# Two layers of graph attention on one core: loading and turning h earlier in the order of issue

## The chip, the cores and the metric

The kernel runs on one core of one Trainium2 chip. The metric is the device time of a launch in microseconds (us). Before the change it was 4149.87 us, the median of three runs from 4149.01 to 4151.54.

A core has engines that each work through a queue of their own in order: TensorE (PE) for matmuls, VectorE (DVE), ScalarE (ACT), GpSimd (POOL), and SyncE (SP), which issues most DMAs here. They wait for one another by semaphores. The kernel fixes the order in each queue itself: an operation's place in the program is its place in its engine's queue.

## The reference, cut to what matters

There are 32 batches of 512 rows by 512 features. Layer 0 adds a graph sum to x and normalises; layer 1 adds masked attention with eight heads and normalises again.

```python
def _L0(x, adj, W, b):
    Wi, Wj = W[:, :512], W[:, 512:]
    mi = einsum('bkd,od->bko', x, Wi); mj = einsum('bkd,od->bko', x, Wj)
    a = adj.astype(x.dtype); deg = a.sum(axis=1)
    return deg[None, :, None] * (mi + b) + einsum('ij,bjo->bio', a, mj)

def _L1(h, adj, ...):                        # 8 heads of 64
    q, k, v = [split_heads(h @ Wx.T + bx) for x in "qkv"]
    scores = einsum('bhqd,bhkd->bhqk', q, k) / 8
    scores = where(adj == 0, -inf, scores)
    out = einsum('bhqk,bhkd->bhqd', softmax(scores), v)
    return merge_heads(out) @ Wo.T + bo

x = layernorm(x + _L0(x, adj, ...))          # this is h
x = layernorm(x + _L1(x, adj, ...))
```

## The kernel before

Each large product is done in 2 by 2 blocks with seven products instead of eight. Such a product is a **piece**; its number i (1 to 7) says which of the seven it is. Pieces 1, 2 and 3 take quarters of the activations as they are; pieces 5, 6, 7 and 4 take differences of quarters (t1 to t4), which GpSimd makes. The kinds of piece are `l0` (layer 0's two products), `v`, `q`, `k`, and `pj` (the output projection). The weights' blocks come from DRAM through a ring of eight tiles: after each piece, `prefetch` issues the load of the tiles that the ring has room for, and that load waits until the piece has read its own.

```python
def piece(kind, b, i, bank):
    ...
        a = {1: (0, 0), 2: (1, 0), 3: (1, 1)}.get(i)
        terms.append((take((name, i)), quarters(*a) if a else T[:, {5: 0, 6: 1, 7: 2, 4: 3}[i]]))
    ...                                       # matmuls into PSUM (L413)
    prefetch()                                # ring loads, issued by SyncE
    ...                                       # the result's way out of PSUM, ACT or DVE
```

In the loop over n, the periods, three batches are under way at once: batch n has layer 0's product and normalisation and then v, q, k; batch n - 1 has its attention; batch m = n - 2 has its projection and second normalisation. Layer 0's result h must be had transposed for v, q and k. From n = 2 on this goes through DRAM: `h_store` writes h (issued by ScalarE), `h_load` reads it back in blocks of 32 columns (four DMAs, issued by SyncE), and `h_turn` transposes inside blocks of 32 by 32 on VectorE. All three work by halves; a half is two of the four groups of 128 rows.

```python
def stats(b, half):                           # DVE: bn_stats, bn_aggr; POOL: three small operations
    for ic in range(2 * half, 2 * half + 2):
        MV[b, ic] = work([P, 5], "mv", 12)
        ln_stats(MV[b, ic], XT[b][:, ic, :])
# apply(b, half): ScalarE scales and shifts the same rows

def h_store(b, half):
    if half == 0:
        HR[b] = dram.tile([N, D], FT, name="hd", bufs=2)
    nc.scalar.dma_start(rows(HR[b])[:, 2 * half:2 * half + 2, :], XT[b][:, 2 * half:2 * half + 2, :])

def h_load(b, half):
    if half == 0:
        HA[b] = work([P, DC, N], "xa", 1).rearrange(...)
    src = HR[b].rearrange("(t p) (c q f) -> q p c t f", p=32, q=4, f=32)
    for q in range(4):
        nc.sync.dma_start(HA[b][32 * q:32 * q + 32, half].rearrange("p c (t f) -> p c t f", f=32),
                          src[q][:, :, 8 * half:8 * half + 8, :])

def h_turn(b, half):
    if half == 0:
        HT[b] = big()
    nc.vector.transpose(HT[b][:, :, Q * half:Q * half + Q], HA[b][:, half])
```

The quarters with second index 0 lie in h's first half. So v 1, v 2, q 1, q 2, k 1 and k 2 need the first turn alone, and the differences `combos(TH, ...)`, hence q 5 and v 5, need both.

A period is cut into eight steps of about equal TensorE time (`by_steps`). Each step begins with the attention of batch n - 1, for half a head pair: scores, exponentials on ScalarE, masks on VectorE, then the values of the step before. After that come the step's pieces, with what is left of the attention dealt out between them: `presum` (sums of exponentials, the first on GpSimd, the next two on VectorE), `invert` (reciprocals on VectorE), `scale`, and `tell` (one row of a check of ranges, called told below).

```python
def scores(b, hp, kc):
    ...                                       # matmuls of k and q (L467)
    nc.scalar.activation(ps, ps, AF.Exp, scale=QSCALE)
    nc.vector.tensor_tensor(e, ps, edge[...], op=OP.mult)     # the mask, L472

def presum(hp, half):
    if half == 0:
        ES[hp] = work([P, 2, N], "es", 1)
        nc.gpsimd.tensor_add(ES[hp], E[0], E[1])              # L478
    else:
        nc.vector.tensor_add(ES[hp], ES[hp], E[half])         # L480
```

With n = 10 the old order gives these steps (worked out from the lists; `combTH` are the differences of h):

```
2  apply(10,0) h_store(10,0) l0.5 add_bo(9,1) pj.4 h_load(10,0) l0.3 stats(10,1) stats(8,0) pj.5
3  h_turn(10,0) apply(10,1) h_store(10,1) v.1 pj.3 stats(8,1) v.2 q.1 h_load(10,1) k.1 apply(8,0) apply(8,1) q.2
4  store(8) k.2 h_turn(10,1) combTH combTH q.5 v.5 q.3 v.3
```

## Time and profile before

| | |
|---|---|
| device time | 4149.87 us, median of 3 |
| span of the profiled execution | 4152.1 us |
| mean granted TensorE clock | 0.953 of full |
| one batch in the middle of the run | about 128 us |
| DMA | 127 GB/s over the span |

The page is read like this. Times are in us. PE is TensorE's matmuls, PEld its weight loads, DVE VectorE, ACT ScalarE, POOL GpSimd, SPq and ACTq the DMA issues of SyncE and ScalarE. In a line of a timeline, an idle time in brackets stands ahead of the operation, and "<-" names what ended it; "issue" means that the profile shows no releaser. A tile named `big` holds turned activations or differences, `ring` a weight block, `mma` and `mmb` are two PSUM banks, `oT` is the attention's output, `xa` h as loaded and not yet turned, `hd` its copy in DRAM.

The costliest groups of instructions by engine:

```profile
L413 PE MATMUL mma<-ring,big 128*128 128x256 f32 x3112 | 770.4, 399 | 74.7 <-issue 70.8
L472 DVE TENSOR_TENSOR e<-sc,edge 128x1024 f32<-128x1024 f32 x512 | 602.5, 1218 | 360.2 <-ACT sc L471 360.2
L382 POOL TENSOR_TENSOR big<-big 128x512 f32<-128x512 f32 x376 | 507.4, 1377 | 28.6 <-ACT big L340 12.0
L413 PE MATMUL mmb<-big,ring 128*128 128x256 f32 x1776 | 451.0, 399 | 44.1 <-POOL big L382 44.1
```

The first number after the bar is the group's busy time in us, the second the mean of one in ns; then the idle time just before the group's members and what ended most of it.

### The profile page before, as it was taken

What the parts mean: (1) busy time and instruction counts of PE and PEld (TensorE: products, weight loads), DVE (VectorE), ACT (ScalarE), POOL (GpSimd) and SP (SyncE); (2) the same over time, 40 slices, a digit from 0 to 9 for tenths busy, and PEclk for the clock granted to TensorE, in tenths of its full rate; (3) what the DMA queues carried; (4) which work ended last, traced back from release to release, by engine and by line L of the source; (5) the groups of instructions that cost most, each with busy time, mean ns of one, the idle gap of its engine ahead of it and who ended that gap; (6) DMA issues with size and microseconds to landing.
All of it is one profiled execution on the core that took longest, in us unless ns stands there. A gap on an engine that the chain in (4) does not pass through costs nothing.

```text
span 4152.1 us, 46000 instructions
## 1 busy us (share of the span) xinstructions
PE 3881.7 (93%) x16426; PEld 2653.3 (64%) x16426; DVE 2695.3 (65%) x3580; ACT 989.1 (24%) x1356; POOL 2027.5 (49%) x1985
## 2 busy tenths in 40 slices
PE   9999999999999999999999999999999999999987
PEld 6666666666666666666666666666666666666653
DVE  4666666667666676666666666666667666666665
ACT  2222222222222222222222222222222222222222
POOL 3545553455544555445554455553455544555432
PEclk9999999999999999999999999999999999999998
DMA  7444445544445344454444444444534445444441
GB/s 236 124 125 119 129 126 132 140 122 124 120 135 140 115 124 125 131 140 125 118 126 131 132 135 122 124 120 135 144 112 125 126 128 142 117 122 128 130 114 39
DMA packets 803720, 529.25 MB, mean 127 GB/s; under 512 B 529568, under 2 KB 626336, under 8 KB 803488
## 3 DMA queue, kind: packets, MB, share of 16 engines
q1 hardware_dynamic: 786912, 494.26, 43.6%
q10 hardware_dynamic: 16320, 31.46, 2.0%
q8 instruction: 135, 2.21, 0.2%
q14 instruction: 97, 0.79, 0.1%
q0 software_dynamic: 256, 0.53, 0.0%
HBM read 453.25 MB, written 72.88 MB: 127 GB/s over the span
## 4 chain that ended last, share of the span: by engine, by line
PE 85%; issue 4%; DVE 4%; ACT 4%; POOL 3%; DMA 0%; SPq 0%; ACTq 0%; POOLq 0%; DVEq 0%
PE mma L413 28%; PE mmb L413 28%; PE sc L467 10%; PE ov L488 10%; PE mmb L311 3%; PE mma L311 3%; ACT xh L282 2%; PE ov L495 2%; DVE e L472 2%; POOL es L478 2%; POOL big L382 1%; ACT sc L471 1%; ACT q L456 1%; DVE rl L510 0%; PE ov L505 0%
## 5 line engine op out<-in xcount | busy, mean ns | idle before, releaser
L471 ACT ACTIVATE sc<-sc 128x1024 f32<-128x1024 f32 x512 | 492.8, 1006 | 1761.0 <-PE sc L467 1757.1
L413 PE MATMUL mma<-ring,big 128*128 128x256 f32 x3112 | 770.4, 399 | 74.7 <-issue 70.8
L472 DVE TENSOR_TENSOR e<-sc,edge 128x1024 f32<-128x1024 f32 x512 | 602.5, 1218 | 360.2 <-ACT sc L471 360.2
L413 PE MATMUL mmb<-ring,big 128*128 128x256 f32 x3144 | 759.4, 392 | 74.7 <-issue 72.2
L413 PEld LDWEIGHTS mma<-ring,big 128*128 128x128 f32 x3112 | 617.4, 200 | 219.3 <-issue 98.2
L413 PEld LDWEIGHTS mmb<-ring,big 128*128 128x128 f32 x3144 | 610.6, 196 | 211.6 <-issue 99.9
L194 POOL TENSOR_TENSOR xlo<-xh,xhi 128x512 fp32r<-128x512 f32 x128 | 215.3, 1692 | 736.6 <-ACT xhi L193 736.6
L382 POOL TENSOR_TENSOR big<-big 128x512 f32<-128x512 f32 x376 | 507.4, 1377 | 28.6 <-ACT big L340 12.0
L467 PE MATMUL sc<-q,k 64*128 64x512 f32 x2048 | 510.0, 616 | 0.0
L488 PE MATMUL ov<-e,v 128*64 128x512 f32 x2048 | 496.9, 606 | 4.2 <-DVE oT L520 4.2
L413 PE MATMUL mma<-big,ring 128*128 128x256 f32 x1808 | 455.0, 397 | 45.4 <-POOL big L382 44.7
L413 PE MATMUL mmb<-big,ring 128*128 128x256 f32 x1776 | 451.0, 399 | 44.1 <-POOL big L382 44.1
L510 DVE RECIPROCAL rl<-ov 128x128 f32<-128x128 f32 x512 | 466.1, 933 | 11.4 <-PE ov L505 5.7
L478 POOL TENSOR_TENSOR es<-e 128x1024 f32<-128x1024 f32 x128 | 301.9, 2359 | 339.9 <-DVE e L472 219.5
L413 PEld LDWEIGHTS mma<-big,ring 128*128 128x128 f32 x1808 | 354.3, 198 | 128.5 <-POOL big L382 51.2
L413 PEld LDWEIGHTS mmb<-big,ring 128*128 128x128 f32 x1776 | 349.2, 199 | 126.5 <-POOL big L382 50.1
L277 POOL TENSOR_SCALAR mv<-mv 128x1 f32<-128x1 f32 x256 | 49.5, 193 | 774.9 <-DVE mv L276 762.3
L480 DVE TENSOR_TENSOR es<-es,e 128x1024 f32<-128x1024 f32 x248 | 357.8, 1443 | 0.0
L488 PEld LDWEIGHTS ov<-e,v 128*64 128x64 f32 x2048 | 124.6, 136 | 344.4 <-issue 271.8
L467 PEld LDWEIGHTS sc<-q,k 64*128 64x128 f32 x2048 | 176.7, 186 | 208.1 <-issue 208.1
L431 DVE TENSOR_TENSOR xh<-xh,mma 128x512 f32<-128x512 f32 x186 | 126.0, 677 | 277.4 <-PE mma L413 276.8
L431 DVE TENSOR_TENSOR xh<-xh,mmb 128x512 f32<-128x512 f32 x186 | 126.0, 677 | 254.9 <-PE mmb L413 254.8
(144 smaller groups left out, 3774.4 us busy)
## 6 DMA issues: line engine op xcount, KB each, us to landing
ring<-wq SPq DMA_DIRECT2D x160, 256.0 KB, 2.7
ring<-wv SPq DMA_DIRECT2D x160, 256.0 KB, 2.6
ring<-wk SPq DMA_DIRECT2D x160, 256.0 KB, 2.8
ring<-wi SPq DMA_DIRECT2D x155, 256.0 KB, 2.8
ring<-wj SPq DMA_DIRECT2D x155, 256.0 KB, 2.7
ring<-wo SPq DMA_DIRECT2D x155, 256.0 KB, 2.7
xh<-in_x_dram SPq DMA_DIRECT2D x32, 1024.0 KB, 5.5
xa<-in_x_dram SPq DMA_DIRECT2D x124, 256.0 KB, 4.0
```

The costliest lines, as they stand in the source:

```text
L194: nc.gpsimd.tensor_sub(lo, xs, hi.bitcast(FT))
L311: nc.tensor.matmul(pm, parts[w][:, jc, :], adjR[:, jc, :], start=(w == 0 and jc == 0), stop=(w == 1 and jc == NC - 1))
L382: nc.gpsimd.tensor_tensor(dst, p, q, op=OP.subtract)
L413: nc.tensor.matmul(pm[:, c * Q:(c + 1) * Q], lhs, rhs, start=first, stop=(kc == 1 and n == len(terms) - 1), skip_group_check=True)
L431: nc.vector.tensor_tensor(d, d, pm, op=OP.add)
L467: nc.tensor.matmul(ps[:, s, :], KT[b, hp // 2][r, hp % 2, kc * P:(kc + 1) * P], QT[b, hp // 2][r, hp % 2, :], start=True, stop=True)
L471: nc.scalar.activation(ps, ps, AF.Exp, scale=QSCALE)
L472: nc.vector.tensor_tensor(e, ps, edge[:, kc:kc + 1, :].to_broadcast([P, 2, N]), op=OP.mult)
L478: nc.gpsimd.tensor_add(ES[hp], E[0], E[1])
L480: nc.vector.tensor_add(ES[hp], ES[hp], E[half])
L488: nc.tensor.matmul(PV[hp][s * HD:(s + 1) * HD, :], V[b][:, kc, c0:c0 + HD], E[kc][:, s, :], start=(kc == 0), stop=(kc == NC - 1))
L510: nc.vector.reciprocal(rl[:, c], pl[:, c])
```

## The change

Only the order of issue changes, for the batches n = 2 to 31. The first load of h stands directly after piece l0 5, so that SyncE reaches it ahead of the ring tiles that piece pj 4 sets free; the second stands after pj 3 instead of after q 1. The first turn stands ahead of piece pj 5 and thus of the next step's masks; the second, and the differences made from it, stand ahead of k 2, and thus of a reciprocal and of GpSimd's sum. The statistics of batch m move behind pj 3. The purpose is to have h turned sooner for v, q and k.

```diff
-                *project(m, 7), z(apply, n, 0), z(h_store, n, 0), l0[5], z(add_bo, n - 1, 1), *project(m, 4), z(h_load, n, 0),
-                l0[3], z(stats, n, 1), z(stats, m, 0), *project(m, 5)]
+                *project(m, 7), z(apply, n, 0), z(h_store, n, 0), l0[5], z(h_load, n, 0), z(add_bo, n - 1, 1), *project(m, 4),
+                l0[3], z(stats, n, 1), z(h_turn, n, 0), *project(m, 5)]
 ...
-            res = [z(h_turn, n, 0), z(apply, n, 1), z(h_store, n, 1), v[1], *project(m, 3), z(stats, m, 1), v[2], q[1],
-                   z(h_load, n, 1), k[1], z(apply, m, 0), z(apply, m, 1), q[2], z(store, m), k[2], z(h_turn, n, 1),
-                   z(combos, TH, n, h, (1, 2)), z(combos, TH, n, h, (3, 4))]
+            res = [z(apply, n, 1), z(h_store, n, 1), v[1], *project(m, 3), z(h_load, n, 1), z(stats, m, 0), v[2], z(stats, m, 1),
+                   q[1], k[1], z(apply, m, 0), q[2], z(apply, m, 1), z(store, m), z(h_turn, n, 1),
+                   z(combos, TH, n, h, (1, 2)), z(combos, TH, n, h, (3, 4)), k[2]]
```

## The prediction

> **What bounds the kernel now.** I began with the page's busy line and then the chain of waits, by engine:

> ```profile
> PE 3881.7 (93%) x16426; PEld 2653.3 (64%) x16426; DVE 2695.3 (65%) x3580; ACT 989.1 (24%) x1356; POOL 2027.5 (49%) x1985
> ...
> PE 85%; issue 4%; DVE 4%; ACT 4%; POOL 3%; DMA 0%; SPq 0%; ACTq 0%; POOLq 0%; DVEq 0%
> ```

> TensorE is the bound, and the other 15% of the chain is waiting that TensorE does. To find where, I read TensorE's timeline for one batch in the middle of the run (columns: start, duration, engine, line, output and inputs, count, and in brackets the idle time before and its releaser):

> ```profile
> 2054.80 1.99 PE L467 MATMUL sc<-q,k 64*128 64x512 f32 x8
> 2056.72 1.94 PE L488 MATMUL ov<-e,v 128*64 128x512 f32 x8
> 2063.37 3.75 PE L413 MATMUL mma<-ring,big 128*128 128x256 f32 x8 [4.71 <-issue]
> 2066.92 2.34 PE L413 MATMUL mmb<-ring,oT 128*128 128x256 f32 x8
> 2069.09 1.89 PE L413 MATMUL mma<-ring,big 128*128 128x256 f32 x8
> ...
> 2076.09 1.99 PE L467 MATMUL sc<-q,k 64*128 64x512 f32 x8
> ...
> 2080.74 1.99 PE L413 MATMUL mma<-big,ring 128*128 128x256 f32 x8
> 2085.67 3.78 PE L413 MATMUL mmb<-big,ring 128*128 128x256 f32 x8 [2.94 <-POOL big L382]
> 2089.25 3.11 PE L413 MATMUL mma<-ring,big 128*128 128x256 f32 x8
> ...
> 2095.74 1.99 PE L467 MATMUL sc<-q,k 64*128 64x512 f32 x8
> ```

> Two holes, 4.71 and 2.94 us. The windows of 130 us around them have TensorE busy 122.35 us, so 7.65 us idle: these two are all the idle time of a batch. The same two stand in every batch from n = 2 on whose timeline I looked at, with the same lengths. The first eight-matmul piece after each takes 3.75 us instead of 1.89. The views by window give the reason (the two columns to read are TensorE's busy time, the first, and PEclk, the granted clock, third from the end of the line):

> ```profile
> 2059.00:2060.00 1.00, 0.00 (x0) 0.00 (x0) 1.00 (x4) 0.68 (x1) 0.81 (x3) 1.00 0.00 0
> 2060.00:2061.00 1.00, 0.00 (x0) 0.00 (x0) 1.00 (x2) 0.00 (x0) 0.84 (x3) 1.00 0.39 150
> 2061.00:2062.00 1.00, 0.00 (x0) 0.00 (x0) 1.00 (x1) 0.00 (x0) 0.27 (x2) 0.50 0.98 373
> ...
> 2066.00:2067.00 1.00, 1.00 (x4) 0.75 (x3) 0.00 (x0) 0.00 (x0) 0.00 (x0) 0.50 0.00 0
> ```

> TensorE stops at 2058.66 (2056.72 + 1.94). At about 2061.0, after 2.3 us of idling, its clock falls to half and stays there until about 2067.8. A hole costs its length and then half of the slow time after it. VectorE is 1.00 busy throughout.

> Next I asked what ends each hole: VectorE's and GpSimd's timelines, and SyncE's queue of DMA issues.

> ```profile
> 2059.76 2.35 DVE L472 TENSOR_TENSOR e<-sc,edge 128x1024 f32<-128x1024 f32 x2
> 2062.03 1.24 DVE L359 STREAM_TRANSPOSE big<-xa 128x1024 f32<-128x1024 f32 x1
> ...
> 2082.68 1.19 DVE L359 STREAM_TRANSPOSE big<-xa 128x1024 f32<-128x1024 f32 x1
> ```
> ```profile
> 2082.05 2.35 POOL L478 TENSOR_TENSOR es<-e 128x1024 f32<-128x1024 f32 x1 [7.57 <-DVE e L472]
> 2084.36 5.04 POOL L382 TENSOR_TENSOR big<-big 128x512 f32<-128x512 f32 x4
> ```
> ```profile
> 2050.20 3.24 SPq L353 DMA_DIRECT2D xa<-hd  x4
> ```

> Hole 1: the turn of h's first half ends at 2063.27 and v's first piece starts at 2063.37; the releaser named "issue" is really this turn. Its data were not late: the four loads issue from 2050.20, and the last (at about 2052.5, 3.9 us to landing) is there at 2056.4. The turn merely stands in VectorE's queue behind two sets of statistics, an add, a told and two masks. Hole 2: the second turn ends at 2083.87, GpSimd is still in its sum of exponentials until 2084.4, then makes t1 (1.27 us), and q's piece 5 starts at 2085.67.

> [...]

> **The change part by part.** No work is added or taken away; the batch's matmuls, DMAs, turns and sums are as many as before. What moves:

> (a) First load: from behind pj 4's ring refill (2049.73) to directly behind l0 5's two (the last ends at 2048.38). It starts at 2048.4 instead of 2050.20 and lands at 2056.4 − 1.8 = 2054.6. The store it waits for was issued at 2044.15, with 2.8 us to landing: done by 2047.0.

> (b) First turn: directly after the statistics of (n, 1), ahead of pj 5's add, the told and the masks. These statistics end at 2057.08. The turn runs 2057.0 to 2058.2, with 2.4 us to spare for its data. TensorE leaves the values at 2058.66, so v 1 needs no wait: **hole 1 goes entirely**, and with it the half clock.

> (c) Statistics of m = n − 2 move behind pj 3. VectorE loses 1.6 us of them ahead of the masks and gains a 1.2 us turn; the masks end at about 2061.7 as before. In step 3 it then has two sums (2 × 1.2), pj 3's add (0.7) and four statistics (3.2): done by about 2067.7, with the next masks due at 2071.3.

> (d) Second load: behind pj 3's refill. v 1 and pj 3 now end at 2058.7 + 2 × 1.73 = 2062.1; h's second half, stored at 2059.71, lands at about 2062.6. The load issues at 2062.6 to 2065.9 and lands by 2068.7.

> (e) Second turn, with TH's differences, ahead of k 2, hence ahead of a reciprocal and of GpSimd's sum. Six pieces of 1.73 from 2058.7 put step 4's scores at 2069.05. Step 2 shows masks ending 4.57 us after the start of scores (2039.60 to 2044.17): 2073.6. Turn until 2074.8, t1 until 2076.1. TensorE meanwhile does scores 1.92, values 1.8, sums 0.96 and k 2 1.73 and wants q 5 at 2075.45. **Hole 2 shrinks to about 0.7 us.** That is well short of the 2.2 us of idling that preceded either fall of the clock, so the half clock doesn't return.

> **The sum.** With scores as marks, steps 3 and 4 take 21.29 + 19.65 = 40.94 us here, and in the batch before, with the PSUM banks swapped, 1927.12 to 1967.41 = 40.29 us; mean 40.6. Unhindered: step 5, with six pieces and no sums, takes 2110.09 − 2095.74 = 14.35; step 4 has one piece less and the sums more, 14.35 − 1.73 + 0.96 = 13.58. Together 27.9. Gain 12.7 us a batch, less the 0.7 that stays, 12.0. Batches n = 2 to 31 have this path: 30 × 12.0 = 360. 4150 − 360 = **3790 us**. The last of the 30 cuts its steps elsewhere (its holes are 6.30 and 3.50 us); I take it as one like the others, an error of a few us at most.

> **The rivals.** *First: the hole at q 5 stays long.* Its chain in (e) is tight: GpSimd's three small operations for each row of m's statistics must be done before ScalarE's two normalisings, which stand in ScalarE's queue ahead of q 2's bias and the exponentials. I reckon them done at 2067.8, k 1's copy at 2068.0; each us of slip is a us of hole. At 1.5 us it costs 0.8 × 30 = 24 more, 3815. At over 2.2 us the clock falls too: some 6 us a batch as before, and the time is about 3950. For it: VectorE and GpSimd lose the idle time that let them catch up. Against it: 3.6 us of slack on VectorE by (c). *Second: another engine becomes the bound.* At 115 us a batch VectorE's 85.5 us are 74% and GpSimd's 64 are 56%; steps 5, 6, 7, 0, 1 and 2 already run without holes at TensorE's full rate, with the same work. I don't expect it. *Third: an early turn blocks VectorE.* If h's first half landed after 2057.0, pj 5's add and the masks would wait behind the turn. There are 2.4 us for it, and a slip of 1 us more would cost only that. *Fourth: ring tiles late behind h's loads.* The refills of pj 4 and l0 3 issue up to 2 us later, but are eight tiles ahead, over 10 us of TensorE time; landing takes about 3 us. Hidden. *Fifth, the other way:* hole 2 vanishes too: 4150 − 30 × 12.7 = 3769.

> **Range and chances.** Between a full removal with a few us more at the ends (3755) and a hole of some 2 us with the clock mostly kept (3850). Both holes must return in full for no gain: faster 0.96, same 0.03, slower 0.01.

> **What would show it.** In the changed kernel TensorE's timeline should have no idle time ahead of v 1, and under 1 us ahead of q 5, named GpSimd's difference; PEclk near 1.00 nearly everywhere; a batch of about 115.6 us; the first turn directly after four statistics and ahead of the masks; GpSimd's differences ahead of its sum. A hole of over 2 us at q 5, PEclk of 0.50 in every batch, or VectorE idle at the first turn until a DMA lands would prove me wrong.

## The result and the profile after

The changed kernel takes **3796.38 us** (median of 4, 3792.98 to 3798.30), the kernel before, in the same series, 4150.39 us. The ratio is 0.9146, 95% interval 0.913 to 0.9162: 354 us or 8.5% less. A second series of the unaltered changed kernel gave 3793.02 us and 0.9147 (0.9134 to 0.9159).

The page of the changed kernel, busy line and chain of waits by engine:

```profile
PE 3736.6 (99%) x16426; PEld 2551.5 (67%) x16426; DVE 2694.1 (71%) x3580; ACT 992.3 (26%) x1356; POOL 2027.6 (53%) x1985
...
PE 92%; DVE 4%; POOL 1%; ACT 1%; DMA 1%; issue 1%; SPq 0%; DVEq 0%; POOLq 0%; ACTq 0%
```

Each engine has as many instructions as before, and VectorE and GpSimd are busy for as long, within 2 us. TensorE is busy 145 us less with the same 16426 matmuls: that is the slow clock gone (mean granted 0.996 after 0.953). The rest is idle time gone. TensorE's timeline over the same two steps of one batch:

```profile
2005.14 1.99 PE L467 MATMUL sc<-q,k 64*128 64x512 f32 x8
2007.06 1.94 PE L488 MATMUL ov<-e,v 128*64 128x512 f32 x8
2008.93 1.99 PE L413 MATMUL mmb<-ring,big 128*128 128x256 f32 x8
...
2019.48 1.99 PE L467 MATMUL sc<-q,k 64*128 64x512 f32 x8
...
2026.67 1.99 PE L413 MATMUL mma<-big,ring 128*128 128x256 f32 x8 [0.55 <-POOL big L382]
...
2033.78 1.99 PE L467 MATMUL sc<-q,k 64*128 64x512 f32 x8
```

The piece v 1 at 2008.93 follows the values without a bracket: hole 1 is gone. Ahead of q 5 stand 0.55 us instead of 2.94, and the piece after it takes 1.99 us instead of 3.78. From the scores of step 3 to those of step 5 it is 28.64 us (40.94 before). The next batch has its q 5 at 2142.69, so a batch takes 116.02 us, 128.0 before.

VectorE's timeline shows what the new order does:

```profile
2007.23 0.18 DVE L276 BATCH_NORM_AGGREGATE mv<-st 128x2 f32<-128x6 f32 x1
2007.41 1.25 DVE L359 STREAM_TRANSPOSE big<-xa 128x1024 f32<-128x1024 f32 x1
2008.58 0.65 DVE L431 TENSOR_TENSOR xh<-xh,mma 128x512 f32<-128x512 f32 x1
...
2021.70 2.36 DVE L472 TENSOR_TENSOR e<-sc,edge 128x1024 f32<-128x1024 f32 x2 [3.52 <-ACT sc L471]
2023.97 1.24 DVE L359 STREAM_TRANSPOSE big<-xa 128x1024 f32<-128x1024 f32 x1
```

The first turn comes directly behind the statistics of its own batch and ends at 2008.66, before TensorE is through with the values at 2009.0. The second comes directly behind the masks, and GpSimd makes its differences at once:

```profile
2025.36 5.07 POOL L382 TENSOR_TENSOR big<-big 128x512 f32<-128x512 f32 x4 [4.48 <-DVE big L359]
2030.38 2.36 POOL L478 TENSOR_TENSOR es<-e 128x1024 f32<-128x1024 f32 x1
```

Before, the sum (L478) stood ahead of the differences (L382). Now GpSimd even waits 4.48 us for the turn, which costs nothing.

### The profile page after: what moved, and what is told of

Read it like the earlier page. It is cut to its first block, busy times and chain, and to the rows that moved or that the text cites. A ratio compares the mean times of both kernels' runs of the same rounds, so it can differ in the third digit from the quotient of the medians.

```text
span 3793.4 us, 46029 instructions
## 1 busy us (share of the span) xinstructions
PE 3736.6 (99%) x16426; PEld 2551.5 (67%) x16426; DVE 2694.1 (71%) x3580; ACT 992.3 (26%) x1356; POOL 2027.6 (53%) x1985
## 4 chain that ended last, share of the span: by engine, by line
PE 92%; DVE 4%; POOL 1%; ACT 1%; DMA 1%; issue 1%; SPq 0%; DVEq 0%; POOLq 0%; ACTq 0%
PE mmb L413 30%; PE mma L413 30%; PE sc L467 12%; PE ov L488 11%; PE mmb L311 3%; PE mma L311 3%; PE ov L495 2%; DVE e L472 2%; POOL big L382 1%; DVE big L359 1%; ACT sc L471 1%; DVE rl L510 0%; PE ov L505 0%; DMA wq<-e 0%; DMA ring<-in_wqT_dram 0%
## 5 line engine op out<-in xcount | busy, mean ns | idle before, releaser
L472 DVE TENSOR_TENSOR e<-sc,edge 128x1024 f32<-128x1024 f32 x512 | 602.5, 1218 | 262.0 <-ACT sc L471 262.0
L413 PE MATMUL mmb<-ring,big 128*128 128x256 f32 x3144 | 733.3, 382 | 3.4 <-issue 3.1
L413 PE MATMUL mma<-ring,big 128*128 128x256 f32 x3112 | 726.3, 382 | 4.2 <-ACT p L420 2.5
L413 PEld LDWEIGHTS mmb<-ring,big 128*128 128x128 f32 x3144 | 592.9, 190 | 132.9 <-issue 29.4
L413 PEld LDWEIGHTS mma<-ring,big 128*128 128x128 f32 x3112 | 586.5, 190 | 135.2 <-issue 27.0
L382 POOL TENSOR_TENSOR big<-big 128x512 f32<-128x512 f32 x376 | 507.8, 1378 | 149.2 <-DVE big L359 129.8
L467 PE MATMUL sc<-q,k 64*128 64x512 f32 x2048 | 509.9, 616 | 0.0
L488 PE MATMUL ov<-e,v 128*64 128x512 f32 x2048 | 496.0, 605 | 4.2 <-DVE oT L520 4.2
L413 PE MATMUL mma<-big,ring 128*128 128x256 f32 x1808 | 431.9, 382 | 8.7 <-POOL big L382 7.7
L413 PE MATMUL mmb<-big,ring 128*128 128x256 f32 x1776 | 424.3, 382 | 8.3 <-POOL big L382 8.3
L413 PEld LDWEIGHTS mma<-big,ring 128*128 128x128 f32 x1808 | 339.1, 190 | 86.5 <-POOL big L382 14.2
L413 PEld LDWEIGHTS mmb<-big,ring 128*128 128x128 f32 x1776 | 333.0, 190 | 85.1 <-POOL big L382 14.3
L478 POOL TENSOR_TENSOR es<-e 128x1024 f32<-128x1024 f32 x128 | 302.2, 2361 | 121.8 <-PE ov L495 108.7
L488 PEld LDWEIGHTS ov<-e,v 128*64 128x64 f32 x2048 | 124.5, 136 | 344.4 <-issue 271.8
L467 PEld LDWEIGHTS sc<-q,k 64*128 64x128 f32 x2048 | 176.7, 186 | 208.1 <-issue 207.8
L326 POOL TENSOR_TENSOR big<-big,deg_r 128x512 f32<-128x512 f32 x124 | 196.9, 1588 | 177.4 <-DVE big L325 177.4
## 6 DMA issues: line engine op xcount, KB each, us to landing
ring<-wq SPq DMA_DIRECT2D x160, 256.0 KB, 2.9
ring<-wv SPq DMA_DIRECT2D x160, 256.0 KB, 3.1
ring<-wk SPq DMA_DIRECT2D x160, 256.0 KB, 2.8
ring<-wi SPq DMA_DIRECT2D x155, 256.0 KB, 2.8
ring<-wj SPq DMA_DIRECT2D x155, 256.0 KB, 2.6
ring<-wo SPq DMA_DIRECT2D x155, 256.0 KB, 2.7
xa<-in_x_dram SPq DMA_DIRECT2D x124, 256.0 KB, 4.0
```

Source lines behind the costliest of these rows:

```text
L326: nc.gpsimd.tensor_tensor(XD[b][:, dc, :], XD[b][:, dc, :], deg_r, op=OP.mult)
L382: nc.gpsimd.tensor_tensor(dst, p, q, op=OP.subtract)
L413: nc.tensor.matmul(pm[:, c * Q:(c + 1) * Q], lhs, rhs, start=first, stop=(kc == 1 and n == len(terms) - 1), skip_group_check=True)
L467: nc.tensor.matmul(ps[:, s, :], KT[b, hp // 2][r, hp % 2, kc * P:(kc + 1) * P], QT[b, hp // 2][r, hp % 2, :], start=True, stop=True)
L472: nc.vector.tensor_tensor(e, ps, edge[:, kc:kc + 1, :].to_broadcast([P, 2, N]), op=OP.mult)
L488: nc.tensor.matmul(PV[hp][s * HD:(s + 1) * HD, :], V[b][:, kc, c0:c0 + HD], E[kc][:, s, :], start=(kc == 0), stop=(kc == NC - 1))
```

## The experiments

The change moves several things at once. My theory: the holes were set by the places of the two turns in VectorE's queue, and of the sum and of two normalisations ahead of the second one's way to q 5. The rival: the loads of h came too late, and their earlier issue is what helped. The parts were therefore undone and done singly. Ratios are to the kernel before.

### The loads alone, and everything but the loads

```diff
 # e1, in the kernel before
-l0[5], z(add_bo, n - 1, 1), *project(m, 4), z(h_load, n, 0),
+l0[5], z(h_load, n, 0), z(add_bo, n - 1, 1), *project(m, 4),
-*project(m, 3), z(stats, m, 1), v[2], q[1], z(h_load, n, 1), k[1],
+*project(m, 3), z(h_load, n, 1), z(stats, m, 1), v[2], q[1], k[1],
 # e2, in the changed kernel: the same two moves undone
```

> The order of before, with only the two loads of h at their new, earlier places. Theory (the turns' places in VectorE's and GpSimd's queues set the holes; the data were there in time already): no gain, 4150 us within 10, both holes of 4.7 and 2.9 us still there. Rival (the loads' earlier issue is what shortens the wait): at least a third of the gain of 354 us, 4030 us or less.

> The changed kernel with both loads of h put back to their old places, behind pj 4 and behind q 1; the turns stay early. Theory: in the changed kernel's timeline the first load would land about 1.9 us later, near 2007.2 against a turn at 2007.4, and the second about 3.5 us later, near 2022.5 against a turn at 2024.0: no loss, 3796 us within 15 (a loss of some tenths of a us a batch if the first landing is late). Rival (the loads matter): one of the turns waits for its data, VectorE stands in front of it, and the time rises by over 40 us.

Measured: e1 4146.58 us, ratio 1.0001 (0.9992 to 1.001); e2 3802.63 us, 0.918 (0.9155 to 0.9205). The loads alone bring nothing, and all the rest without them brings nearly the whole gain. In e1 both holes stand as they stood:

```profile
1932.63 3.75 PE L413 MATMUL mmb<-ring,big 128*128 128x256 f32 x8 [4.71 <-issue]
1954.94 3.78 PE L413 MATMUL mma<-big,ring 128*128 128x256 f32 x8 [2.94 <-POOL big L382]
```

In e2 both loads issue later, and in a batch in the middle of the run both turns start without waiting for them. SyncE's queue and then VectorE's timeline:

```profile
1769.04 3.46 SPq L353 DMA_DIRECT2D xa<-hd  x4
...
1785.01 3.76 SPq L353 DMA_DIRECT2D xa<-hd  x4
```
```profile
1775.91 1.25 DVE L359 STREAM_TRANSPOSE big<-xa 128x1024 f32<-128x1024 f32 x1
...
1792.48 1.24 DVE L359 STREAM_TRANSPOSE big<-xa 128x1024 f32<-128x1024 f32 x1
```

The last of the first load's four issues starts at 1771.5 and none takes over 3.5 us to land, so the data are there by 1775.0, 0.9 us before their turn at 1775.91; the second has 1.2 us to spare. Three turns of the run do wait for their load: 0.74 and 0.29 us in the third and fourth batch on this path, and 4.24 us in the last. The first of these costs TensorE 0.50 us, the last 1.71 us (VectorE's line, then TensorE's):

```profile
3663.81 1.25 DVE L359 STREAM_TRANSPOSE big<-xa 128x1024 f32<-128x1024 f32 x1 [4.24 <-DMA xa<-hd]
3665.69 1.94 PE L488 MATMUL ov<-e,v 128*64 128x512 f32 x8 [1.71 <-DVE oT L520]
```

That is some 2 us of the 354. Another six batches of e2 are 0.85 us longer, by a stall in step 5 whose cause is open; e4 below, with the early loads, has five of these stalls and the changed kernel one. In the totals, e2's interval overlaps that of the changed kernel (0.913 to 0.9162). The rival falls.

### The first turn's place

```diff
 # e3, in the changed kernel: the turn at the head of step 3, behind its masks
-l0[3], z(stats, n, 1), z(h_turn, n, 0), *project(m, 5)]
+l0[3], z(stats, n, 1), *project(m, 5)]
-res = [z(apply, n, 1), ...
+res = [z(h_turn, n, 0), z(apply, n, 1), ...
 # e4, in the changed kernel: only the statistics of m ahead of the turn
-l0[3], z(stats, n, 1), z(h_turn, n, 0), *project(m, 5)]
+l0[3], z(stats, n, 1), z(stats, m, 0), z(h_turn, n, 0), *project(m, 5)]
-z(h_load, n, 1), z(stats, m, 0), v[2]
+z(h_load, n, 1), v[2]
```

> The changed kernel with only the first turn back behind the next step's masks (the statistics of batch m stay at their new place). The masks then end about 1.2 us earlier than with the turn ahead of them, at 2010.9 in the changed kernel's timeline, the turn at 2012.1, and v 1 would start 3.2 us after TensorE stopped at 2008.9. Theory: hole 1 comes back with about 3.2 us, the clock falls to half as after 2.2 us of idling before, some 3 us more: 30 batches x 6.2 = 186, about 3980 us. If the clock stayed full: 30 x 3.2 = 96, 3892 us. Rival (hole 1 was closed by the load or by the statistics' move): under 3830 us.

> The changed kernel with the first two statistics of batch m back ahead of the first turn, which stays ahead of pj 5's add and the masks. They take 1.6 us of VectorE, so the turn ends at about 2010.2 in the changed kernel's timeline, 1.2 us after TensorE is free. Theory: a hole of 1.2 us a batch with the clock full throughout, 30 x 1.2 = 36, 3832 us, PEclk still near 1.00. Rival (any hole of over 1 us costs the clock as well): about 3 us more a batch, 3920 us.

Measured: e3 3920.54 us (0.9473, 0.9443 to 0.9504), e4 3843.45 us (0.9282, 0.9256 to 0.9307). The holes are 3.12 and 1.35 us, close to the 3.2 and 1.2 expected: each instruction ahead of the turn costs its own time. e4 pays 1.6 us of statistics less the slack of some 0.3. In e4 no piece after the hole of 1.35 us is slow; 30 x 1.35 = 40 us, and 47 were measured. The rest lies at least in part in the five stalls (4 us) and in the last batch, whose hole ahead of v 1 is 4.68 us here and 3.09 in the changed kernel.

e3 is neither of the two totals I had set down, 3980 with the clock falling everywhere and 3892 with it nowhere. Its timeline tells why: the hole always has the same length, but what follows differs. Four successive batches:

```profile
1353.18 3.44 PE L413 MATMUL mmb<-ring,big 128*128 128x256 f32 x8 [3.12 <-issue]
...
1473.83 1.97 PE L413 MATMUL mma<-ring,big 128*128 128x256 f32 x8 [3.12 <-issue]
...
1593.00 1.97 PE L413 MATMUL mmb<-ring,big 128*128 128x256 f32 x8 [3.12 <-issue]
...
1712.18 3.75 PE L413 MATMUL mma<-ring,big 128*128 128x256 f32 x8 [3.12 <-issue]
```

The bracket is 3.12 us each time, the piece 3.44, 1.97, 1.97 and 3.75 us. Of the 29 batches n = 2 to 30, 14 have a piece of 2.6 us or more and 15 one of 1.96 or 1.97. So the clock doesn't follow the length of the hole alone; where the hole lies counts too (see the last section).

### What stands ahead of q 5

```diff
 # e5, in the changed kernel: the differences behind k 2, hence behind GpSimd's sum
-z(h_turn, n, 1), z(combos, TH, n, h, (1, 2)), z(combos, TH, n, h, (3, 4)), k[2]]
+z(h_turn, n, 1), k[2], z(combos, TH, n, h, (1, 2)), z(combos, TH, n, h, (3, 4))]
 # e6, in the changed kernel: all of m's normalisations ahead of q 2
-z(apply, m, 0), q[2], z(apply, m, 1), z(store, m),
+z(apply, m, 0), z(apply, m, 1), q[2], z(store, m),
```

> The changed kernel with the differences t1 to t4 behind GpSimd's sum of exponentials; the second turn stays early on VectorE. GpSimd's sum would run from 2024.1 to 2026.4 in the changed kernel's timeline and t1 until 2027.7, with q 5 wanted at 2026.1. Theory: hole 2 grows from 0.55 to about 1.65 us and the clock stays full: 30 x 1.1 = 33, 3829 us. Rival (a hole of 1.65 us already brings the half clock): about 3 us more a batch, 3920 us. Second rival (GpSimd's sum is not what counts): 3796 us.

> The changed kernel with all four normalisings of batch m ahead of q 2 on ScalarE, as before the change; everything else stays. The last rows' statistics leave GpSimd at 2020.9 in the changed kernel's timeline, so q 2's bias ends at about 2022.6 and the exponentials, now at 2020.66, start at about 2022.5; masks, turn and t1 follow 1.9 us later. Theory: hole 2 is 2.4 us, and if the clock stays full that is 30 x 1.9 = 57, 3853 us; with the half clock about 3940 us. Rival (ScalarE's order plays no part, VectorE has room): 3796 us.

Measured: e5 3831.82 us (0.9243, 0.9229 to 0.9257), e6 3891.66 us (0.9391, 0.9377 to 0.9406). e5's hole is 1.80 us, and in all of the batches n = 2 to 30 the piece behind it takes 1.99 us, so the clock stays full; 30 x (1.80 - 0.55) = 37.5 us, measured 35. GpSimd's sum is one part of the old hole 2, worth 1.25 us a batch.

e6 is another part, and an unspoken one of the change: two normalisations moved behind q 2. ScalarE's timeline in e6:

```profile
1942.61 0.81 ACT L282 ACTIVATE xh<-xh,mv 128x512 f32<-128x512 f32 x1 [0.34 <-POOL mv L279]
1943.33 0.81 ACT L456 ACTIVATE q<-mmb,bq_c 128x256 f32<-128x256 f32 x2
1944.05 1.93 ACT L471 ACTIVATE sc<-sc 128x1024 f32<-128x1024 f32 x2
```

ScalarE waits for GpSimd's small operations on the last row's statistics, and the exponentials behind it start 2.86 us after the step's scores (1941.19), in the changed kernel 1.18 us after (2020.66 against 2019.48). Masks, turn and differences follow that much later. The hole is 2.25 us, 1.7 more than 0.55. Here too the clock doesn't fall in every batch, and the time lies between my two totals, 3853 and 3940. The views by window of two batches of e6, one after the other, with TensorE's busy time first and the granted clock third from the end:

```profile
1831.00:1832.00 1.00, 0.00 (x0) 0.00 (x0) 0.74 (x1) 0.00 (x0) 0.95 (x1) 1.00 0.81 227
1832.00:1833.00 1.00, 0.64 (x3) 0.58 (x4) 0.00 (x0) 0.00 (x0) 0.92 (x2) 1.00 0.10 35
...
1949.00:1950.00 1.00, 0.00 (x0) 0.00 (x0) 0.44 (x1) 0.00 (x0) 1.00 (x1) 0.97 0.80 234
1950.00:1951.00 1.00, 0.93 (x2) 0.84 (x3) 0.00 (x0) 0.00 (x0) 0.92 (x2) 0.50 0.03 8
```

The hole that ends at 1832.37 is followed by full speed, that which ends at 1950.07 by half speed, at equal length. Of the batches n = 2 to 30, 25 have a slowed piece and 4 have none.

### Each half of the change alone

```diff
 # e9, in the kernel before: first load and first turn as in the change, and
-v[1], *project(m, 3), z(stats, m, 1), v[2], ...
+v[1], *project(m, 3), z(stats, m, 0), z(stats, m, 1), v[2], ...
 # e10, in the changed kernel: the first half undone
-l0[5], z(h_load, n, 0), z(add_bo, n - 1, 1), *project(m, 4), l0[3], z(stats, n, 1), z(h_turn, n, 0), *project(m, 5)]
+l0[5], z(add_bo, n - 1, 1), *project(m, 4), z(h_load, n, 0), l0[3], z(stats, n, 1), z(stats, m, 0), *project(m, 5)]
-res = [z(apply, n, 1), ... z(stats, m, 0), v[2],
+res = [z(h_turn, n, 0), z(apply, n, 1), ... v[2],
```

> The kernel before with only the first half of the change: first load and first turn early, the statistics of batch m behind pj 3; the second load, the second turn, the normalisations and GpSimd's sum in the old order. Hole 1 goes, hole 2 stays with about 2.9 us. Theory of fixed costs (a hole costs its length and always the slow clock after it, as in the kernel before): 4147 - 30 x 7.2 = 3931 us. [...] 3796 + 30 x (2.4 + about 1) = 3898 us, with the first piece after the hole taking 1.99 us in some batches and up to 3.8 in others.

> The kernel before with only the second half of the change: second load, second turn and differences early, two normalisations behind q 2; the first load, the first turn and the first statistics of batch m in the old order. Hole 1 stays with 4.7 us, hole 2 shrinks to about 0.55. [...] the clock falls in every batch: 3796 + 30 x 7.0 = 4006 us, PEclk about 0.97. The gains of this run and of the one with the first turn alone then add up to more than the 354 us of both together [...].

Measured: e9 3950.09 us (0.9527, 0.9513 to 0.9542), e10 3996.51 us (0.9633, 0.9618 to 0.9648). The gains are 198 and 151 us, together 349, about the 354 of both. For e9 neither of my totals holds: 3931 us had the clock fall in every batch, 3898 us in some only, as it had in e3. The hole ahead of q 5 did not stay at 2.9 us:

```profile
1979.99 3.59 PE L413 MATMUL mmb<-big,ring 128*128 128x256 f32 x8 [3.39 <-POOL big L382]
```

All of the batches n = 2 to 30 have 3.39 or 3.40 us, and in all but the first of them the piece after it takes 3.5 us or more. In the kernel before, hole 1 had held TensorE back, so that VectorE, GpSimd and ScalarE had more time ahead of step 4; without it the second chain shows its full length. The exponentials of step 4 start 2.85 us after their scores in e9 (1972.81 against 1969.96), much as in e6, and 2.41 us in the kernel before (2078.50 against 2076.09): that is the difference between 3.39 and 2.94. The parts from the runs above give nearly that length: 0.55 + 1.25 (sum) + 1.70 (normalisations) = 3.50. The reciprocal that also stood ahead of the second turn adds nothing, for the turn ends at 1978.19, while GpSimd is in its sum until 1978.72. So the first half alone brings 6.8 us a batch (128.0 to 121.2), though hole 1 with its slow clock had cost 7.3 (the steps of 21.29 and 21.98 us against 14.35).

My inequality falls too: I had the gains add up to more than the whole, because the clock was to fall in part of e9's batches only; with a fall in each, they were to add up to the same. With 3.39 us it falls in 28 of 29. e10 has holes of 4.71 and 0.55 us and a slow piece in each batch, as expected.

### Taking the last 0.55 us away

```diff
 # e7, in the changed kernel: second turn and differences in step 3, ahead of step 4's masks
-q[1], k[1], z(apply, m, 0), q[2], z(apply, m, 1), z(store, m), z(h_turn, n, 1), combos, combos, k[2]]
+q[1], k[1], z(apply, m, 0), z(h_turn, n, 1), combos, combos, q[2], z(apply, m, 1), z(store, m), k[2]]
 # e8, in the changed kernel: the second turn in two instructions
-nc.vector.transpose(HT[b][:, :, Q * half:Q * half + Q], HA[b][:, half])
+for j in range(2) if half else (None,):
+    c = slice(0, DC) if j is None else slice(2 * j, 2 * j + 2)
+    nc.vector.transpose(HT[b][:, c, Q * half:Q * half + Q], HA[b][:, half, c])
 # e11, as e7, and in the last batch alone the first turn ahead of l0[3]
 # e12, the changed kernel unaltered
```

> The changed kernel with the second turn and the differences moved one step earlier, ahead of q 2 and thus ahead of step 4's masks. The load lands at about 2019.5 in the changed kernel's timeline, VectorE is idle from 2018.2 to 2021.7, so the turn runs at about 2019.6 to 2020.8 and t1 is there at 2022.2, 4 us before q 5 wants it. Theory: the remaining hole of 0.55 us (0.7 us of the step) goes, 30 x 0.7 = 21, 3775 us. Rival (the turn waits for the load and holds up the masks behind it, or GpSimd's differences come before the statistics' small operations): no gain or a loss, 3796 us or more.

> The changed kernel with the second turn cut into two instructions of half the columns, so that t1, which needs only the first, can start about 0.6 us earlier. Theory: the remaining hole of 0.55 us nearly goes, 30 x 0.55 = 16, 3780 us. Rival (the two halves take longer than one and GpSimd starts no earlier): 3796 us.

> The run with the second turn and the differences in step 3, and in the last batch alone the first turn ahead of l0 3 as well, where the changed kernel still has a hole of 3.09 us ahead of v 1 and a slow piece after it. Theory: 4.5 us less than the 3768 us of that run, about 3763 us, and no hole of over 1.1 us ahead of the last batch's v 1. Rival: the last batch's turn waits for its load, in front of the masks, and nothing is won.

> The changed kernel once more, unaltered, beside the run before it, so that the two can be compared on the same chip: 3796 us within 5.

| | us | ratio to before |
|---|---|---|
| e12, the changed kernel again | 3793.02 | 0.9147 (0.9134 to 0.9159) |
| e8, turn halved | 3780.96 | 0.9123 (0.9111 to 0.9136) |
| e7, turn in step 3 | 3767.57 | 0.9089 (0.9077 to 0.9102) |
| e11, as e7, last batch mended | 3768.31 | 0.9086 (0.9073 to 0.9098) |

e7 beats both kernels by an interval clear of theirs, 25 us under e12 where 21 were expected; q 5 has no idle time ahead of it any more. VectorE's timeline in e7:

```profile
1888.19 1.25 DVE L359 STREAM_TRANSPOSE big<-xa 128x1024 f32<-128x1024 f32 x1 [1.01 <-DMA xa<-hd]
1890.70 2.36 DVE L472 TENSOR_TENSOR e<-sc,edge 128x1024 f32<-128x1024 f32 x2 [1.26 <-ACT sc L471]
```

With this order (e7 and e11) the second turn waits for its load in each of the batches n = 2 to 30, here 1.01 us and over the run 0.2 to 2.4 us. VectorE had nothing else to do, and the masks still start 2.2 us after their scores, as ever. After the turn the masks still wait 1.26 us for their exponentials, so by my estimate a load that lands more than that later would hold them up: in this version the change's earlier second load probably matters. That wasn't tried. e8's median lies 12 us under e12's, but their intervals just touch; in its timeline no idle time is left ahead of q 5, and step 4 takes 13.76 us instead of 14.30 (2011.44 to 2025.20). e11 removes the last batch's hole ahead of v 1 in the timeline (3.09 us, then 0.65 ahead of pj 3); the 4.5 us that this should bring are too few for the measurement, and its median isn't below e7's.

## Why the prediction was right, by its steps

**Hole 1** was to go entirely: it did. Its cause, the turn's place behind ready data, is shown by e2 (later loads, the hole stays closed but for 0.50 us in one batch) and e3 and e4 (later turns, holes of the expected length).

**Hole 2** was to shrink to about 0.7 us: the idle time is 0.55, and step 4 takes 14.30 us, 0.72 more than the unhindered 13.58. The chain held at every joint: exponentials 1.18 us after the scores, masks until 4.58 us after them, statistics of m done 13.0 us into step 3, where 12.9 had been reckoned, and VectorE idle for 3.52 us after them, where 3.6 of slack had been.

**The half clock** was not to return: PEclk is 0.996 on the mean, and the clock's record shows full speed without a break from 67.6 to 3638.0 us.

**The sum** was 12.0 us a batch and 360 in all; measured 12.0 (128.0 to 116.02) and 354. A part of the missing 6 us lies in the last batch, which the prediction had taken as one like the others: a hole of 3.09 us stays ahead of its v 1, with a slow piece after it. The prediction's "batch of about 115.6 us" was a slip: 128.0 less 12.0 is 116.0. Likewise its 85.5 and 64 us for VectorE and GpSimd belong to a window of 130 us, not to a batch; the page has 71% and 53%.

**Parts (a) and (d)**, the earlier loads, were described rightly as giving data more time; e1 and e2 show that this time was hardly needed: without it some 2 us are lost in all.

**The rivals.** The first, a longer hole at q 5, is what e5 and e6 make. Its figure for a hole of over 2.2 us, 3950 us, was too high for e6's 2.25 (3892). It took 6 us a batch from the kernel before. In e6 the hole costs 1.7 us more than 0.55, and a fall of the clock lasts 3.413 us each time and so costs at most 1.7; four batches have none. VectorE as the bound, an early turn that blocks, and late ring tiles don't show: no idle time but the 0.55 us stands on TensorE's timeline of that batch. (Whether the one stall of 0.85 us in step 5 elsewhere in the run is a late ring tile stays open.)

## What to carry to other kernels

Where an engine takes its queue in order, as VectorE did here (before the change, data of 2056.4 were turned at 2062.03, behind the masks), ask of each wait on the critical engine whether the awaited instruction lacked data or only its turn; compare its data's landing with its start. If the data were there, move the instruction ahead of what isn't urgent; the transfers' own places counted for some 2 us of 354 here. And follow the chain over all engines: here two normalisations on ScalarE, off the path by their own result, were worth more than the sum that stood visibly in front (1.70 and 1.25 us), and closing one hole let the next show its full length.

## What the runs showed of the hardware that was not expected

In these runs TensorE's clock fell by where a hole lay in time as well as by its length. In the batches n = 2 to 30, holes of 1.35 and 1.80 us never cost the clock; 2.25 us did in 25 of 29, 3.12 us in 14 of 29 and 3.39 us in 28 of 29; 4.71 us did in all, and so did the 2.94 us of the kernel before.

```profile
1468.81:1472.22 3.41, 1.89 (x10) 0.44 (x8) 3.38 (x7) 2.67 (x4) 1.71 (x5) 1.00 0.08 29
1472.22:1475.63 3.41, 1.80 (x9) 1.63 (x10) 2.61 (x3) 0.00 (x0) 0.00 (x0) 1.00 0.41 154
...
1707.74:1711.15 3.41, 1.32 (x8) 0.15 (x4) 3.41 (x6) 2.10 (x3) 1.24 (x4) 1.00 0.05 20
1711.15:1714.56 3.41, 2.38 (x6) 1.96 (x7) 2.04 (x2) 0.00 (x0) 0.00 (x0) 0.50 0.37 140
```

Cut into such stretches, the trace before the change (without the first 250 and the last 40 us) has 61 at whose end the clock fell: TensorE was idle for at least 1.99 us in each. In the 961 that began at full speed and kept it, it was idle for at most 1.60 us. In all 14 traces these are 236 with at least 1.96 us and 14123 with at most 1.95. A stretch at half speed was followed by a second one where TensorE idled for 0.62 us or more in it, and by full speed where it idled for 0.52 us or less (0.77 and 0.12 before the change). The ends of matmuls are modelled in the profile, so the last digit is not to be relied on; the limits are those of these traces.

In kernels that lose the clock in every batch or nearly so, whole batches can also last a multiple of those 3.413 us. Two batches take 256.0 us before the change (75.0 x 3.413) and 242.3 in e9 (71.0), one batch of e10 122.88 (36.0). e6, which loses it in each of its last 15 batches, isn't quite at a multiple: 119.40 us (34.98). After a fall, full speed returned at a point of the grid in every trace, wherever the hole ended. From that and the 3.413 us between the points I estimate that a small gain ahead of such a hole can be swallowed until the next point; I haven't tested it. It would be a reason to measure a change at a hole by removing the hole, rather than by shortening it a little.
